# Two attention blocks on one core: the place of the softmax inverses, of one weight copy and of the output fetches

## Chip, core and metric

The kernel runs on one core of a Trainium2 chip. The metric is the device time of one execution in microseconds, as the median of several runs.

## The reference

Four images of 32 x 32 positions with 768 channels go through two layers of the same kind. All is in float32. In each layer:

```
x = x + attention(group_norm(x, groups=32))
attention:  q, k, v = x @ Wqkv (+ bias in layer 1), 12 heads of 64
            scores = scale * q k^T + rel_h[q_row, k_row] + rel_w[q_col, k_col]
            out = softmax(scores) v;   out @ Wproj + bproj
```

`rel_h` and `rel_w` are products of q with a small table of relative positions. Layer 1 scales q twice and has biases on q, k and v.

## The kernel before, in words

**Tiling.** The work is eight images (layer, image), each of six pairs of heads, each pair of eight steps. So there are 48 pairs g = 0 to 47, and pair number `pair` = g % 6 within its image. A step handles 128 query positions of both heads: a tile of scores of 128 x 1024 per head. Channels and positions are held transposed (channels on partitions) in 128 x 512 tiles.

**One step n of pair g**, in program order, with the lines of the profile:

- SP first issues what was put off from earlier steps (weight loads L131, stores L637); in pair 4 of an image also the loads of the next image (L117); in steps 4 and 6 `fetch` brings output weights `wo` (L580) and operands `res` (L600).
- GpSimd adds the two position terms of step n+2 into `sc` (L461).
- TensorE makes the scores of step n+1 (L475, eight records of the profile), VectorE adds them to `sc` and takes the row's maximum (L484), ACT takes the exponential and its sum (L488).
- SP reads back transposed weights of an earlier quarter (`pt<-td`, L526).
- VectorE transposes the two tiles of step n in 32 x 32 blocks (L515, `turn`), into tiles `tb`, of which there are three. After every second step (a quarter of the pair) SP writes them to DRAM (`td<-tb`, L518).
- VectorE takes the inverse of the sums of step n+1 (L495); GpSimd multiplies head 0's tile by it (L499), ACT head 1's (L501). This is `divide`.
- In pair 4 VectorE applies the norm to the next image's tiles (`apply`, L228).
- `take` issues the step's share of other TensorE work from a list `todo`: the projections of the next pair to q and k (L268) and values (L376), and output projections (L621).
- One function of the list `last`, if there is one: eight ACT copies of position terms into `rel` (L431), which read tiles `t` of the same pool as `res` (four tiles).
- After step 6 TensorE weighs the values with quarters 0 and 1 (L545, `weigh`), after step 2 with quarters 2 and 3 of the pair before.

**Projection of q and k.** In 39 of the 48 pairs (not the first of an image, nor pair 1) it is a product of 2 x 2 blocks with fewer block products. Of the weights, `w0` holds A11 (upper 64 rows, `TOP`) and A12 (`LOW`), `w1` A21 and A22, each in six chunks. ACT and GpSimd make S1 and S2 in `w3` (L324, L327, L328) and overwrite A21 (L329), in the steps before. Four units follow: unit 0 (six chunks, A11 and A12) in step 0, unit 1 (three chunks, S2, its two halves on the two halves of the array) and unit 2 (six chunks, S1 and S4) in step 1, unit 3 in step 3. Unit 1 finds chunks 0 to 2 of S2 in the place of A11's chunks 0 to 2, and unit 2 finds S4 = A12 - S2 in A12's place. So A11 and A12 are overwritten after unit 0 has read them, by the copy L336 on VectorE and the subtraction L337 on GpSimd:

```
def sum_weights_last(g):
    w0, w3 = w_of[g, 0], w_of[g, 3]
    nc.vector.tensor_copy(w0[TOP, :3], w3[LOW, :3])
    nc.gpsimd.tensor_tensor(w0[LOW], w0[LOW], w3[LOW], ALU.subtract)
```

It is called when unit 0's six chunks are issued, behind the reading of their result: ACT's copy into k (L296) and VectorE's addition into q (L243). Results of the units, of the position products (L408, copied to `t` by ACT, L418), of the weighing (L554, L557) and of the output products lie in two tiles of PSUM that are used in turn.

**What sets the order.** Each engine works through its own instructions in program order, and so does SP's DMA queue; waits are on semaphores. The order is written out by hand: the shares of each step stand in a list, for instance 6, 9, 0, 6, 6, 6, 0, 12 chunks for steps 0 to 7, and `first` says how many of them come ahead of the transposes.

Of the kernel before, what the change touches and what calls it, by code (L numbers as in the profile page):

```python
# [44 lines left out]
ALU = mybir.AluOpType  # L45
# [6 lines left out]
NC = C // P  # L52
NT = S // P
# [13 lines left out]
def attention_blocks(ctx: ExitStack, tc: tile.TileContext, a: dict, out: bass.AP):  # L67
    nc = tc.nc
# [27 lines left out]
    NPAIR = NI * NP  # L96

    w_of, wo_of = {}, {}
# [138 lines left out]
    def plain(g):  # L237
        return g % NP == 0 or g == 1
# [8 lines left out]
    def project_in(g, unit):  # L247

        im, pair = divmod(g, NP)
        xs, ys = x_of[im], y_of[im]  # L250
        if unit == 0:
            for which in range(2):
                tag = "qk"[which]
                qk_of[g, which] = qkpool.tile([P, S], FP, tag=tag, name=f"{tag}_{g}")
        if plain(g):
            which, i = divmod(unit, 2)
            w, x = 2 * [w_of[g, which]], xs[i * NC : (i + 1) * NC]
        else:
            w0, w1, w3 = w_of[g, 0], w_of[g, 1], w_of[g, 3]
            w, x = (  # L260
                ((w0, w0), xs[:NC]), ((w0, w3[:, 3:]), ys[NC:]),
                ((w3, w0), xs[NC:]), ((w1, w1), ys[:NC]),
            )[unit]
        t = ps_m.tile([P, 2, HALF], FP, tag="m", name=f"pj_{g}_{unit}")
        for c in range(len(x)):
            for a in range(2):
                rows = slice(a * D, (a + 1) * D)
                nc.tensor.matmul(  # L268
                    t[:, a, :], lhsT=w[a][rows, c, :], rhs=x[c][rows, :],
                    start=(c == 0), stop=(c == len(x) - 1),  # L270
                )
            if c < len(x) - 1:
                yield True

        q = [
            qk_of[g, 0][:, i * HALF : (i + 1) * HALF].rearrange("p (m a) -> p m a", a=4)
            for i in range(2)
        ]
        k = qk_of[g, 1].rearrange("p (a m) -> p a m", a=4)
        k = [k[:, :, i * P : (i + 1) * P] for i in range(2)]  # L280
        u = [t[:, a, :].rearrange("p (m a) -> p m a", a=4) for a in range(2)]
        t = [x.rearrange("p m a -> p a m") for x in u]
        bias = [None, None]
        if images[im][0]:
            bias = [bqkv[:, which, pair : pair + 1] for which in range(2)]
        if plain(g):
            to = k[i]
            if which == 0:
                to, t = q[i], u
            if images[im][0] == 0:  # L290
                nc.scalar.copy(to, t[0])
            else:
                nc.scalar.activation(to, t[0], AF.Identity, bias=bias[which])
            add(to, t[1], to)
        elif unit == 0:
            nc.scalar.copy(k[0], t[0])  # L296
            add(q[0], u[1], k[0].rearrange("p a m -> p m a"), bias[0])
            sum_weights_last(g)
        elif unit == 1:
            add(k[0], t[0], k[0])  # L300
            add(k[0], t[1], k[0])
        elif unit == 2:
            add(k[1], t[0], k[0])
            add(q[1], u[1], k[1].rearrange("p a m -> p m a"), bias[0])
        else:
            add(k[1], t[0], k[1], bias[1])
            add(k[0], t[0], k[0], bias[1])
            nc.vector.tensor_tensor(k[0], k[0], t[1], ALU.subtract)
        if unit in ((0, 1) if plain(g) else (0, 2)):
            (later if g else mid).append(lambda: positions(g, 1 if unit else 0))  # L310
        if g + 1 < NPAIR:
            if unit == (1 if plain(g) else 2):
                later.append(lambda: load_w(g + 1, 0))
            if unit == 3:
                early.append(lambda: load_w(g + 1, 1))
        yield True

    def sum_weights(g):

        w0, w1 = w_of[g, 0], w_of[g, 1]  # L320
# [12 lines left out]
    def sum_weights_last(g):  # L333

        w0, w3 = w_of[g, 0], w_of[g, 3]
        nc.vector.tensor_copy(w0[TOP, :3], w3[LOW, :3])  # L336
        nc.gpsimd.tensor_tensor(w0[LOW], w0[LOW], w3[LOW], ALU.subtract)  # L337

    def sum_input(im, n):

# [111 lines left out]
    sc_of, st_of, tb_of, pt_of, attn_of = {}, {}, {}, {}, {}  # L452
# [15 lines left out]
    def scores(g, n):  # L468
# [13 lines left out]
        for h in range(2):  # L482
# [7 lines left out]
                accum_out=st[:, 1, h : h + 1],  # L490
            )

    def divide(g, n):
        st = st_of[g, n]
        nc.vector.reciprocal(st[:, 2, :], st[:, 1, :])  # L495
        for h in range(2):
            sc = sc_of[g, n, h].rearrange("p k j -> p (k j)")
            if h == 0:
                nc.gpsimd.tensor_scalar(sc, sc, st[:, 2, h : h + 1], 1.0, ALU.mult, ALU.mult)  # L499
            else:  # L500
                nc.scalar.activation(sc, sc, AF.Copy, scale=st[:, 2, h : h + 1])  # L501

    def turn(g, n):

        quarter, j = divmod(n, 2)  # L510
        for h in range(2):
            if j == 0:
                tb_of[h] = tbpool.tile([P, HW, 2, HW], FP, tag="tb", name=f"tb_{g}_{n}_{h}")
            tb = tb_of[h]
            nc.vector.transpose(tb[:, :, j, :], sc_of[g, n, h])  # L515
            if j == 1:
                td = dram2.tile([P, S * 2], FP, tag=f"td{h}", name=f"td_{g}_{n}_{h}")
                nc.sync.dma_start(out=td, in_=tb.rearrange("p k n i -> p (k n i)"))  # L518
                (behind if quarter % 2 else behind2).append(
                    lambda queue=None, h=h, td=td: read_back(g, quarter, h, td, queue)  # L520
                )

    def read_back(g, quarter, h, td, queue=None):
        pt = ptpool.tile([P, 4, NT, 2 * HW], FP, tag=f"pt{h}", name=f"pt_{g}_{quarter}_{h}")
# [48 lines left out]
    def fetch(upto):  # L573

        while fetched[0] <= min(upto, len(parts) - 1):
            im, p, o, i = parts[fetched[0]]
            c0, c1 = cuts(im)[p : p + 2]
            if i == 0:
                w = wopool.tile([P, NC // 2, P], FP, tag="wo", name=f"wo_{im}_{p}_{o}")
                nc.sync.dma_start(  # L580
                    out=w[:, : c1 - c0, :],
                    in_=a[f"wo{images[im][0]}"][o][:, c0 * P : c1 * P].rearrange(
                        "p (c o) -> p c o", o=P
                    ),
                )
                for c in range(c0, c1):
                    wo_of[im, o, c] = w[:, c - c0, :]
            fetched[0] += 1
        while fetched[1] <= min(upto, len(parts) - 1):
            im, p, o, i = parts[fetched[1]]  # L590
            l, b = images[im]
# [21 lines left out]
    def project_out(im, p, o, i):  # L613
        l, b = images[im]
        end = im + 1 == NI
# [23 lines left out]
            nc.sync.dma_start(out=dst, in_=to)  # L639
        if i == 1 and (im, p, o, i) in place:  # L640
            if end and o > 1:
                fetch(place[im, p, o, i] + 4)
        yield True

# [37 lines left out]
    with tc.manual_schedule(engines=ENGINES):  # L682
# [19 lines left out]
        run(later)  # L702
        biases(0, 0)
        scores(0, 0)
        divide(0, 0)
        biases(0, 1)

        units = [(g, n) for g in range(NPAIR) for n in range(NT)]
        for at, (g, n) in enumerate(units):
            im, pair = divmod(g, NP)  # L710
# [18 lines left out]
            if pair == 4 and not end:  # L729
                if n == 0:  # L730
                    make_room(im + 1)
                for c in range(3 * n - 3, 3 * n) if 1 <= n <= 4 else ():
                    load_x(im + 1, c % NC, c // NC)
            if (im, pair) == (B - 1, 4) and n in (5, 7):
                (load_table if n == 5 else scale_table)(1)
# [1 line left out]
            early, later = later, early  # L737

            upto = 4 * (pair % 3) + 3
            if n in (4, 6) and (im, pair) >= (0, 3):  # L740
                upto -= 6 - n
                fetch(place[((im, 0) if pair >= 3 else (im - 1, 1)) + divmod(upto, 2)])

            ask = [divmod(g + 3, NP)] if n == 1 else []
            if im == 0 and pair < 3:
# [13 lines left out]
            if pair == 3 and n in stages and not end:  # L759
                stages[n]()  # L760
            share = shares[n]
            first = 3 if n == NT - 1 else 2 if end and pair == NP - 1 and n in (3, 4) else 0
            first = min(first, share)
            take(todo, first)
            share -= first
# [1 line left out]
            if at + 1 < len(units):  # L767
                divide(*units[at + 1])
            if pair == 4 and not end:
                for c in {2: (0, 1), 4: (2, 3), 6: (4, 5, 6, 7), 7: range(8, NX)}.get(n, ()):  # L770
                    if n == 7 and c % 2 == 0:
                        take(todo, 3)
                        share -= 3
                    apply(c % NC, c // NC)
# [2 lines left out]
                    combine = sum_weights(g + 2)  # L777
                combine[n - 6]()
            take(todo, share)
            if last:  # L780
                last.pop(0)()
            if pair == NP - 2 and n == 7 and not end:
                sum_input(im + 1, -1)
# [73 lines left out]
```

## Time and profile before

| what | value |
|---|---|
| median of three runs | 3571.03 us (3569.75 to 3577.24) |
| the profiled execution | 3578.79 us, of which 3577.0 us are the span of its instructions |
| ACT, busy | 1986.2 us |
| scores L475, eight records a step | 3072 records, 746.3 us |
| products L268 | 4140 records, 938.7 us |
| copy L336 | 39 copies, 25.2 us |
| inverse L495 | 384, mean 125 ns |
| transposes L515 | 768, mean 1222 ns |
| additions L461 on GpSimd | 768, mean 2083 ns |
| granted clock of TensorE | 0.994 of full speed |
| DMA | 1051.55 MB, mean 294 GB/s |

Busy times and waits are totals over the span. A line of a timeline gives the start, the duration, the engine, the line of the kernel, and at its end in brackets the idle time before it and what ended it. `PEld` is the loading of weights into TensorE, `SPq` an instruction of SP's queue. Matmuls are pipelined, so the times between their starts say more than their durations. Times within a pair are counted from the start of its step 0, and a step starts with the first of its eight score matmuls.

### The profile page before, as it was taken

To read this page: it belongs to the slowest core of one execution; us is meant where nothing else is said; L and a number is where in the kernel's file an instruction comes from. 1 tells how busy PE (TensorE), PEld (TensorE's weight loads), DVE (VectorE), ACT (ScalarE), POOL (GpSimd) and SP (SyncE) were. 2 spreads that over 40 slices of the span, in tenths; PEclk is the share of its full clock that TensorE was granted. 3 is DMA by queue.
4 is the path that set the end of the run, shared out by engine and by line. 5 is a ranking of instruction groups with operands and counts; after the bars stand their busy time and mean duration, and the time that the engine had idled before them with its cause. 6 is when DMAs were issued, how large, how long until landed. Compare 5 with 4: busy or idle time off the path is not lost.

```text
span 3577.0 us, 56189 instructions
## 1 busy us (share of the span) xinstructions
PE 3417.6 (96%) x20652; PEld 1897.0 (53%) x20652; DVE 2592.0 (72%) x4011; ACT 1986.2 (56%) x3958; POOL 2492.1 (70%) x1510
## 2 busy tenths in 40 slices
PE   6899999999999999999999999999999999999999
PEld 4455555555555556555555555555555555555554
DVE  4687867777777777777777777777766677776776
ACT  3565565555555556555655566555654555555552
POOL 3877686676967669676786667876678666786663
PEclk9999999999999999999999999999999999999999
DMA  3688978888788887888888788878988789887878
GB/s 118 244 287 319 328 278 302 318 309 316 276 316 317 300 307 272 319 293 306 292 308 304 281 316 301 306 285 292 308 307 301 271 290 330 299 291 276 296 288 289
DMA packets 531220, 1051.55 MB, mean 294 GB/s; under 512 B 143872, under 2 KB 206848, under 8 KB 481792
## 3 DMA queue, kind: packets, MB, share of 16 engines
q1 hardware_dynamic: 476448, 1020.53, 79.3%
q10 hardware_dynamic: 54496, 27.43, 2.6%
q8 instruction: 162, 2.65, 0.3%
q14 instruction: 114, 0.93, 0.1%
HBM read 572.73 MB, written 475.10 MB: 293 GB/s over the span
## 4 chain that ended last, share of the span: by engine, by line
PE 52%; DVE 17%; DMA 15%; ACT 5%; issue 5%; POOL 4%; SPq 2%; ACTq 0%; DVEq 0%; POOLq 0%
PE pj L268 13%; PE av L545 12%; PE s L475 10%; PE o L621 10%; DVE tb L515 8%; DMA td<-tb 7%; DMA pt<-td 7%; PE pv L376 6%; DVE sc L484 5%; ACT sc L501 2%; PE tp L408 2%; POOL sc L461 2%; DVE x L228 1%; POOL x L346 1%; POOL x L351 1%
## 5 line engine op out<-in xcount | busy, mean ns | idle before, releaser
L461 POOL TENSOR_TENSOR sc<-rel,rel 128x1024 f32<-128x1024 f32 x768 | 1546.1, 2083 | 42.6 <-DMA rel<-tdr 35.8
L488 ACT ACTIVATE sc<-sc,sm 128x1024 f32<-128x1024 f32 x768 | 880.1, 1147 | 662.8 <-DVE sm L484 660.0
L499 POOL TENSOR_SCALAR sc<-sc,sm 128x1024 f32<-128x1024 f32 x384 | 435.5, 1134 | 934.4 <-DVE sm L495 926.4
L484 DVE CUSTOM_DVE_ANT_0 sc<-s,sc 128x1024 f32<-128x1024 f32 x768 | 908.7, 1220 | 214.1 <-PE s L475 164.9
L268 PE MATMUL pj<-x,w 64*128 64x512 f32 x4140 | 938.7, 598 | 99.3 <-DVE w L336 60.1
L515 DVE STREAM_TRANSPOSE tb<-sc 128x1024 f32<-128x1024 f32 x768 | 913.0, 1222 | 122.9 <-DMA td<-tb 122.8
L545 PE MATMUL av<-pt,v 128*64 128x256 f32 x6144 | 717.3, 385 | 41.0 <-DMA pt<-td 41.0
L475 PE MATMUL s<-k,q 64*128 64x512 f32 x3072 | 746.3, 596 | 6.2 <-DVE sm L484 6.1
L501 ACT ACTIVATE sc<-sc,sm 128x1024 f32<-128x1024 f32 x384 | 441.0, 1148 | 556.8 <-DVE sm L495 556.8
L268 PEld LDWEIGHTS pj<-x,w 64*128 64x128 f32 x4140 | 415.7, 189 | 600.2 <-issue 444.4
L545 PEld LDWEIGHTS av<-pt,v 128*64 128x64 f32 x6144 | 446.0, 138 | 341.4 <-DMA pt<-td 60.3
L376 PE MATMUL pv<-wv,x 64*128 64x256 f32 x4608 | 514.1, 376 | 0.0
L376 PEld LDWEIGHTS pv<-wv,x 64*128 64x128 f32 x4608 | 446.4, 187 | 92.2 <-issue 29.9
L621 PE MATMUL o<-attn,wo 128*128 128x512 f32 x1080 | 480.5, 598 | 8.5 <-DVE attn L554 3.5
L475 PEld LDWEIGHTS s<-k,q 64*128 64x128 f32 x3072 | 289.2, 187 | 297.0 <-issue 272.7
L431 ACT COPY rel<-t 32x64 f32<-32x64 f32 x1504 | 362.9, 241 | 15.4
L621 PEld LDWEIGHTS o<-attn,wo 128*128 128x128 f32 x1080 | 199.9, 190 | 285.9 <-issue 234.4
L418 ACT COPY t<-tp 128x512 f32<-128x512 f32 x188 | 110.0, 585 | 191.5 <-PE tp L408 137.0
L243 DVE TENSOR_TENSOR k<-pj,k 128x512 f32<-128x512 f32 x173 | 116.8, 684 | 136.8 <-PE pj L268 94.9
L346 POOL TENSOR_TENSOR x<-x,x 64x512 f32<-64x512 f32 x144 | 182.6, 1288 | 43.9 <-ACT x L348 28.8
L391 DVE TENSOR_TENSOR v<-pv,v 128x256 f32<-128x256 f32 x192 | 81.4, 424 | 91.2 <-ACT v L388 88.0
L488 ACT ACTIVATION_READ_ACCUMULATOR sc<-sc,sm 128x1 f32 x768 | 143.2, 187 | 0.0
(54 smaller groups left out, 1516.9 us busy)
## 6 DMA issues: line engine op xcount, KB each, us to landing
td<-tb SPq DMA_DIRECT2D x384, 1024.0 KB, 5.6
pt<-td SPq DMA_DIRECT2D x382, 1024.0 KB, 8.0
w<-in_wqk SPq DMA_DIRECT2D x96, 384.0 KB, 3.5
tdr<-t ACTq DMA_DIRECT2D x94, 256.0 KB, 4.6
x<-in_x SPq DMA_DIRECT2D x84, 256.0 KB, 6.6
part<-res SPq DMA_DIRECT2D x84, 256.0 KB, 5.5
res<-part SPq DMA_DIRECT2D x84, 256.0 KB, 6.9
wv<-in_wv SPq DMA_DIRECT2D x24, 768.0 KB, 12.1
```

The costliest lines, as they stand in the source:

```text
L268: nc.tensor.matmul(t[:, a, :], lhsT=w[a][rows, c, :], rhs=x[c][rows, :], start=(c == 0), stop=(c == len(x) - 1),)
L376: nc.tensor.matmul(t[:, a, k, :], lhsT=xs[i // 2 * NC + c][rows, at * P : (at + 1) * P], rhs=w[rows, c, :], start=(c == 0), stop=(c == NC ...
L431: nc.scalar.copy(rel[of, :, j, :], t[of, j, :, at : at + HW])
L461: nc.gpsimd.tensor_tensor(sc.rearrange("p (a k) (u l) -> p a l (k u)", a=4, l=8), rel0[:, h, :].unsqueeze(1).unsqueeze(2).to_broadcast(shape),
L475: nc.tensor.matmul(ps[h][:, cols], lhsT=q[rows, n * P : (n + 1) * P], rhs=k[rows, cols], start=True, stop=True,)
L484: nc.vector.tensor_tensor_reduce(out=sc, in0=ps[h], in1=sc, scale=-scale, scalar=BIG, op0=ALU.add, op1=ALU.min, accum_out=st[:, 0, h : h + 1],
L488: nc.scalar.activation(sc, sc, AF.Exp, bias=st[:, 0, h : h + 1], scale=-1.0, accum_out=st[:, 1, h : h + 1],)
L499: nc.gpsimd.tensor_scalar(sc, sc, st[:, 2, h : h + 1], 1.0, ALU.mult, ALU.mult)
L501: nc.scalar.activation(sc, sc, AF.Copy, scale=st[:, 2, h : h + 1])
L515: nc.vector.transpose(tb[:, :, j, :], sc_of[g, n, h])
L545: nc.tensor.matmul(av[rows, at * 2 * P : (at + 1) * 2 * P], lhsT=v_of[g][:, k, rows], rhs=pt_of[g, quarter, h][:, :, k, :], start=(k == 0) ...
L621: nc.tensor.matmul(t, lhsT=wo_of[im, o, c], rhs=attn_of[im * NP + c, i], start=(c == c0), stop=(c == c1 - 1),)
```

## The change

Five things are moved; no arithmetic is added or removed. The weights are fetched by a function of their own.

- The inverse of step n+1 is taken between the two transposes of step n, no longer behind both.
- The copy of half of S2 over A11 is issued when three of unit 0's six chunks are, and those three now come ahead of step 0's transposes. The subtraction on GpSimd stays where it was.
- Output weights are fetched in step 2 (both of the pair), operands in steps 4 and 5, in place of both in 4 and 6.
- In step 3 two functions of `last` are run in place of one.
- In pair 4 the next image's tiles are loaded 6, 3 and 3 in steps 1, 2 and 4 (before: 3 each in 1, 2, 3, 4), and the norm is applied to 3, 1, 3 and 5 of them in steps 2, 4, 6, 7 (before: 2, 2, 4, 4).

```
@@ project_in
+            if c == 2 and unit == 0 and not plain(g):
+                nc.vector.tensor_copy(w0[TOP, :3], w3[LOW, :3])
...
         elif unit == 0:
             nc.scalar.copy(k[0], t[0])
             add(q[0], u[1], k[0].rearrange("p a m -> p m a"), bias[0])
-            sum_weights_last(g)
+            nc.gpsimd.tensor_tensor(w0[LOW], w0[LOW], w3[LOW], ALU.subtract)
@@ divide, turn
+    def invert(g, n):
+        st = st_of[g, n]
+        nc.vector.reciprocal(st[:, 2, :], st[:, 1, :])
+
     def divide(g, n):
         st = st_of[g, n]
-        nc.vector.reciprocal(st[:, 2, :], st[:, 1, :])
...
+            if h == 0 and g * NT + n + 1 < NPAIR * NT:
+                invert(*divmod(g * NT + n + 1, NT))
@@ main loop
-                for c in range(3 * n - 3, 3 * n) if 1 <= n <= 4 else ():
+                for c in {1: range(NC), 2: range(6, 9), 4: range(9, NX)}.get(n, ()):
                     load_x(im + 1, c % NC, c // NC)
...
-            if n in (4, 6) and (im, pair) >= (0, 3):
-                upto -= 6 - n
-                fetch(place[((im, 0) if pair >= 3 else (im - 1, 1)) + divmod(upto, 2)])
+            if n in (2, 4, 5) and (im, pair) >= (0, 3):
+                upto -= 2 if n == 4 else 0
+                (fetch_weights if n == 2 else fetch)(place[((im, 0) if pair >= 3 else (im - 1, 1)) + divmod(upto, 2)])
...
-            first = 3 if n == NT - 1 else 2 if end and pair == NP - 1 and n in (3, 4) else 0
+            first = 3 if n == NT - 1 or n == 0 and g + 1 < NPAIR and not plain(g + 1) else 2 if end and pair == NP - 1 and n in (3, 4) else 0
...
-                for c in {2: (0, 1), 4: (2, 3), 6: (4, 5, 6, 7), 7: range(8, NX)}.get(n, ()):
-                    if n == 7 and c % 2 == 0:
+                for c in {2: (0, 1, 2), 4: (3,), 6: (4, 5, 6), 7: range(7, NX)}.get(n, ()):
+                    if n == 7 and c % 2:
...
-            if last:
+            for k in range(min(len(last), 2 if n == 3 else 1)):
                 last.pop(0)()
```

More of the change, by code (lines that the diff above doesn't have):

```diff
@@ L331, in sum_weights @@
         return first, second
[L333 to L337, printed above, removed]
     def sum_input(im, n):
@@ L571, in attention_blocks, with fetch_weights @@
     fetched = [0, 0]
-    def fetch(upto):
+    def fetch_weights(upto):
         while fetched[0] <= min(upto, len(parts) - 1):
@@ L588, in fetch @@
             fetched[0] += 1
+    def fetch(upto):
         while fetched[1] <= min(upto, len(parts) - 1):
@@ L641, in project_out @@
             if end and o > 1:
+                fetch_weights(place[im, p, o, i] + 4)
                 fetch(place[im, p, o, i] + 4)
@@ L704, in attention_blocks @@
         scores(0, 0)
+        invert(0, 0)
         divide(0, 0)
```

## The prediction

> **What bounds the kernel now.** I read the page first, then the table of waits, then one ordinary pair of heads (g = 13) instruction by instruction, then the stretches in which the granted clock falls.
>
> ```profile
> PE 3417.6 (96%) x20652; PEld 1897.0 (53%) x20652; DVE 2592.0 (72%) x4011; ACT 1986.2 (56%) x3958; POOL 2492.1 (70%) x1510
> ```
>
> TensorE is the bound, and no other engine is above 72%. Its work is not changed here, so only its gaps can be won. The table of waits (total us, times, longest us) names two that recur:
>
> ```profile
> PEld pj L268 <- DVE w L336: 92.4, 39, 5.2
> ...
> PE pj L268 <- DVE w L336: 60.1, 39, 4.4
> ...
> PE av L545 <- DMA pt<-td: 41.0, 34, 2.7
> ```
>
> The first two lines are one wait, seen at the weight load and at the matmul: the product of unit 1 waits for the copy of half of S2 over A11 (L336). The third is the weighing of the values in step 6, which waits for the transposed weights to come back from DRAM. The TensorE timeline of pair 13 shows what the first is worth:
>
> ```profile
> 1018.42 1.88 PE L475 MATMUL s<-k,q 64*128 64x512 f32 x8
> 1021.66 8.00 PE L268 MATMUL pj<-x,w 64*128 64x512 f32 x36 [1.36 <-DVE w L336]
> 1029.49 1.06 PE L408 MATMUL tp<-tab,q 64*128 64x128 f32 x16
> ```
>
> Starts are the measure. Step 0 of this pair (8 + 24 records) takes 6.97 us, 0.218 us a record; so the products could start at 1018.42 + 8 x 0.218 + 0.01 = 1020.17. They start at 1021.66: 1.49 us lost, not 92.4/39 = 2.37, since a weight load would run ahead. VectorE and GpSimd at that time:
>
> ```profile
> 1015.87 2.37 DVE L515 STREAM_TRANSPOSE tb<-sc 128x1024 f32<-128x1024 f32 x2
> 1018.16 0.12 DVE L495 RECIPROCAL sm<-sm 128x2 f32<-128x2 f32 x1
> 1019.97 1.05 DVE L243 TENSOR_TENSOR q<-pj,k 128x512 f32<-128x512 f32 x1 [1.69 <-ACT k L296]
> 1021.05 0.56 DVE L336 COPY w<-w 64x384 f32<-64x384 f32 x1
> ```
>
> ```profile
> 1014.28 4.01 POOL L461 TENSOR_TENSOR sc<-rel,rel 128x1024 f32<-128x1024 f32 x2
> 1018.38 1.12 POOL L499 TENSOR_SCALAR sc<-sc,sm 128x1024 f32<-128x1024 f32 x1
> 1019.59 1.81 POOL L337 TENSOR_TENSOR w<-w,w 64x768 f32<-64x768 f32 x1
> ```
>
> The copy stands behind a chain: both transposes, inverse, ACT's multiplication, ACT's copy of k, the addition into q.
>
> The wait in step 6: it starts at +49.47 us of the pair and takes 8.87 us where nothing is late (pair 19). Over all pairs the steps 6 sum to 73 us above that: about 38 in the 40 ordinary pairs, 35 in the seven pairs (4, 10, ..., 40) that load the next image. Excess and landing agree: pair 13's second `pt` of quarter 1 lands 27.83 us after step 3's start and the excess is 1.94; pair 19's lands at 25.88, excess 0. What stands before it on SP's queue:
>
> ```profile
> 1047.39 7.41 SPq L447 DMA_DIRECT2D rel<-tdr  x8
> 1054.91 0.39 SPq L131 DMA_DIRECT2D w<-in_wqk  x1
> 1055.34 0.43 SPq L580 DMA_DIRECT2D wo<-in_wo  x1
> 1055.81 0.90 SPq L600 DMA_DIRECT2D res<-part  x2
> 1056.76 0.98 SPq L526 DMA_DIRECT2D pt<-td  x2
> ```
>
> **The change, part by part.** The orders of TensorE's and GpSimd's instructions are the same in both kernels; those of VectorE, ACT and SP differ.
>
> *Copy of the half (39 pairs).* It now waits for the third product of unit 0 and stands before the transposes. That product's last record starts 1.82 + 11 x 0.218 = 4.22 us into step 0 and takes 0.59, so the copy can start at +4.87; VectorE's L484s end at +4.50. It costs nothing new (0.39 to 2.74 us, median 0.50, in the rows of L336), only its place: waiting behind it are the transposes, the inverse and what depends on them. Here a rule speaks against the place. The Trainium skill (SBUF — State Buffer, Who interferes with whom) says that a VectorE copy in a 2-port mode and a GpSimd instruction exclude each other, and the later one blocks fully. The rows agree: 2742 ns in pair 2, across two L461s. At +4.87 GpSimd is in its second L461 (+4.78 to +6.84; some 1.1 us earlier once the inverse of the step before is early, so to about +5.75). By the median row the copy ends at +5.4, by the rule at +6.05; I take the rule. Transpose +7.3, inverse +7.4, ACT's multiplication +8.5, k +9.1, q +10.2, L337 (L499, then itself) +10.4. Unit 1 starts free at +8.7, unit 2 at +11.3 (it needs q's buffer and L337): covered by 0.9 us. The position products at +16.6 need unit 1 evacuated, at about +16.2: 0.4 us of cover, partly eaten. So 1.4 of the 1.49 us: 29 pairs x 1.4 = 40 us. In the seven pairs that start an image, GpSimd's two L461s end near +8.8; by the rule the copy ends at +7.1 and L337 at +12.1, 0.8 too late: 7 x 0.7 = 5 us (by the median row 10). Pairs 1 to 3 wait for GpSimd's L337 anyway: 2 us. Sum 47; bounds 25 and 56.
>
> *Inverse between the transposes (384 x 0.125 us).* It passes one transpose of 1.22 us: ACT and GpSimd get it some 1.1 us earlier; the second transpose waits for the second exponential's sum, 0 to 0.3 us per step by pair 13's rows. TensorE waits for neither; the gain is inside the numbers above. In step 6 the inverse no longer stands behind the transpose that waits for a `tb` buffer (122.8 us in 41 waits), so the next GpSimd additions are out of the way when the norm is applied.
>
> *Weights in step 2, operands in 4 and 5, both rel copies in step 3.* Ahead of `pt` one weight DMA goes: 0.43 us of SP and 192 KB, at the 235 GB/s that follows there 0.8 us. Against it the later second transpose of step 3, 0.25. The two `res` of step 5 stand behind `pt` and before `td` of quarter 2 (0.5 MB, 1.5 to 2.1 us): that makes the `tb` wait longer, for `pt` of quarter 2 is not needed until step 2 of the next pair. In step 2 the weights find SP idle. ACT's eight more copies in step 3 (8 x 0.25 = 2 us) delay the exponential and T in step 4 by about 1 us, under VectorE's 1.5 us of idle time there. Landing 0.5 us earlier (bounds +0.3 later, 0.8 earlier): 12 us in some 28 pairs that wait more than that, 4 in the seven; bounds -8 and 22.
>
> *Loads and the norm (seven pairs).* Loads 6, 3, 0, 3 in place of 3, 3, 3, 3: the three that stand before quarter 1's `pt` remain. Three L228 in step 2: alone 0.52 us, but 2.26 beside an L461 (rows of L228). With the inverse early they meet both L461s and hold back the evacuation L554 to about +31.8 (now +28.6), which unit 3 needs at +30.5: 1.3 us lost, 9 us in all (bounds 0 and 12). In step 6 three L228 in place of four, with GpSimd mostly done: step 7 is 14.4 us in five of these pairs and 15.7 in pair 4, against 12.4 undisturbed; I take 10 of these 12 us back. The wait in step 6 also costs clock:
>
> ```profile
> 1720.00:1723.00 3.00, 0.89 (x4) 0.42 (x6) 0.26 (x1) 0.75 (x2) 0.49 (x1) 0.92 1.09 427
> 1723.00:1726.00 3.00, 3.00 (x16) 1.66 (x14) 0.47 (x1) 0.00 (x0) 0.00 (x0) 0.51 0.98 407
> ```
>
> The seventh column is the granted clock: 3.4 us at half, 1.7 us lost, in six of the seven pairs; pair 4, with 2.2 us of wait, keeps it. I take 3 us back of 10. Last, in pairs before an image's first, unit 3 waits 0.5 us in step 4 for ACT's L418, behind GpSimd's sums: 3 us.
>
> **Sum**: 47 + 12 + 4 - 9 + 10 + 3 + 3 = 70 us. The profiled execution took 3578.8 (3577.0 of span); the median shown is 3571.0, 0.2% less, and the difference is not in any row. 3571 - 70 = 3501.
>
> **Rivals.**
> (1) *GpSimd keeps the copy out*: in every pair it waits to +7.1 or beyond. For: the row of 2742 ns, and the rule. Against: after the second L461 GpSimd has only L499, which needs the inverse behind the copy. Then 0.7 us a pair, and the rest as above: 47 becomes 27; 3521, with the applied norm at its worse bound 3530.
> (2) *The wait for `pt` goes too*: its queue empties by more than I count (SP's issues of 1.2 us each behind `td` show back-pressure), and step 6 gives 30 us more, with the clock 7 more: 3464.
> (3) *Slower: the `res` of step 5 share the DMA engines with `pt` of quarter 1 rather than follow it.* They are issued about 1 us after it and 9 us before it lands; shared, 0.5 MB at 235 GB/s is 2.1 us on 40 pairs, 84 us: 3585. It decides from 1.75 us (70/40) on. Against: all landings here are in order of issue (`w`, `wo`, `res`, `pt`, `td`).
> (4) *It does nothing*: what TensorE gains in step 1 comes back in step 6. Against: that chain starts with step 3's transposes, which move along with TensorE. About 3568.
>
> **Chances.** The sum as worked out (3480 to 3520) 0.52; rival 1 (to 3560) 0.23; rival 2 0.13; rival 4 0.05; rival 3 0.07. Range 3460 to 3545: it cuts off the far ends of rivals 1 and 2, and 3 and 4. A measurement of this kernel tells about 0.2% (7 us) from no change: faster 0.88, same 0.05, slower 0.07.
>
> **What would show it.** Right: no wait of L268 for the copy but in pairs 1 to 3; step 1 near 10.5 us in place of 11.96; quarter 1's `pt` landing half a us earlier after step 3; a longer wait of L515 for `td`; step 3 of the loading pairs longer than 6.87, their step 7 near 12.4. Wrong: a wait of L268 for L337, L243 or L336 in ordinary pairs, or a step 6 above 10.4 us on average.

## The result and the profile after

The changed kernel takes 3511.37 us (median of four runs, 3505.53 to 3515.57) against 3571.8 us before (four runs; the 3571.03 further up is of three): a ratio of 0.9827, 95% interval 0.9808 to 0.9846. Its profiled execution takes 3509.05 us, of which 3507.3 are the span. The profiled execution of before was the slowest of its runs, so the spans differ by 69.7 us and the medians by 60.

The engine row of the page after:

```profile
PE 3404.6 (97%) x20652; PEld 1906.9 (54%) x20652; DVE 2640.3 (75%) x4011; ACT 1992.0 (57%) x3958; POOL 2489.6 (71%) x1510
```

TensorE is busy about as long as before (3417.6 us) in a shorter span. VectorE is busy 48 us longer although it has the same 4011 instructions: some of them now take longer (the copies by 13 us in sum, the inverses by 12, the norm and the transposes by 9 each). From the table of waits after (total us, times, longest us):

```profile
DVE sm L495 <- ACT sc L488: 172.4, 269, 6.3
...
DVE tb L518 <- DMA td<-tb: 143.8, 43, 6.9
...
PEld av L550 <- DMA pt<-td: 46.5, 46, 2.6
...
PE av L550 <- DMA pt<-td: 22.8, 22, 2.1
```

```profile
PEld pj L268 <- DVE w L274: 10.3, 3, 4.3
...
PE pj L268 <- DVE w L274: 7.8, 3, 3.5
```

The copy (L336 before, L274 now) is waited for 3 times in place of 39, in pairs 1 to 3. TensorE's wait for `pt` fell from 41.0 to 22.8 us. VectorE waits longer for the second exponential's sum and for a free `tb`. TensorE in pair 13:

```profile
1010.45 1.88 PE L475 MATMUL s<-k,q 64*128 64x512 f32 x8
1012.17 7.89 PE L268 MATMUL pj<-x,w 64*128 64x512 f32 x36
1019.89 1.11 PE L408 MATMUL tp<-tab,q 64*128 64x128 f32 x16
```

The products start 1.72 us after step 1's scores, 3.24 before, and have no gap ahead of them. The 36 records follow each other in 7.89 us in place of 8.00. VectorE and GpSimd in the same time:

```profile
1008.14 1.28 DVE L274 COPY w<-w 64x384 f32<-64x384 f32 x1 [0.16 <-PE pj L268]
1009.45 1.25 DVE L518 STREAM_TRANSPOSE tb<-sc 128x1024 f32<-128x1024 f32 x1
1010.62 0.12 DVE L495 RECIPROCAL sm<-sm 128x2 f32<-128x2 f32 x1
1010.67 1.22 DVE L518 STREAM_TRANSPOSE tb<-sc 128x1024 f32<-128x1024 f32 x1
1012.43 1.06 DVE L243 TENSOR_TENSOR q<-pj,k 128x512 f32<-128x512 f32 x1 [0.55 <-ACT k L299]
```

```profile
1005.19 4.02 POOL L461 TENSOR_TENSOR sc<-rel,rel 128x1024 f32<-128x1024 f32 x2
1010.85 1.12 POOL L502 TENSOR_SCALAR sc<-sc,sm 128x1024 f32<-128x1024 f32 x1 [1.64 <-DVE sm L495]
1012.05 1.81 POOL L301 TENSOR_TENSOR w<-w,w 64x768 f32<-64x768 f32 x1
```

The two L461s end at 1009.21 and the copy at 1009.42, 5.94 us into the pair. What is behind it (inverse, L301, q) is just early enough. On SP's queue in the same pair no output weights (`wo`) stand ahead of quarter 1's `pt` any more, and two `res` follow it:

```profile
1045.00 0.38 SPq L131 DMA_DIRECT2D w<-in_wqk  x1
1045.43 0.91 SPq L608 DMA_DIRECT2D res<-part  x2
1046.38 0.99 SPq L531 DMA_DIRECT2D pt<-td  x2
1047.47 1.45 SPq L608 DMA_DIRECT2D res<-part  x2
```

To see where the time went, the trace is cut at the first score record of each step, for all 48 pairs. Ordinary are the 21 pairs with nothing special; loading are pairs 4, 10, ..., 46 (the last of these eight loads nothing); pre-image are the seven before an image's first, with the plain projection; image-first are pairs 6, 12, ..., 42. The mean us of a step, before and after, and the change of the sum over the class:

| step | class | before | after | sum, us |
|---|---|---|---|---|
| 1 | ordinary (21) | 11.96 | 10.37 | -33.2 |
| 1 | loading (8) | 11.95 | 10.33 | -12.9 |
| 1 | image-first (7) | 11.87 | 10.74 | -7.9 |
| 3 | loading | 6.87 | 7.93 | +8.5 |
| 4 | pre-image (7) | 12.80 | 13.10 | +2.1 |
| 5 | pre-image | 6.90 | 8.03 | +7.9 |
| 6 | ordinary | 10.15 | 9.31 | -17.6 |
| 6 | loading | 13.33 | 12.13 | -9.6 |
| 7 | loading | 13.99 | 13.18 | -6.5 |

The other classes and steps, with pairs 0 to 3 and 47, sum to within 1 us of nothing. These are single executions, and step 6 scatters: between two kernels that do not differ there, its sum changed by up to 3.8 us over the ordinary pairs and by up to 7.4 over the loading pairs. The other rows repeat within some 2 us.

### The profile page after: what moved, and what is told of

Read it like the earlier page. It is cut to its first block, busy times and chain, and to the rows that moved or that the text cites. A ratio compares the mean times of both kernels' runs of the same rounds, so it can differ in the third digit from the quotient of the medians.

```text
span 3507.3 us, 56203 instructions
## 1 busy us (share of the span) xinstructions
PE 3404.6 (97%) x20652; PEld 1906.9 (54%) x20652; DVE 2640.3 (75%) x4011; ACT 1992.0 (57%) x3958; POOL 2489.6 (71%) x1510
## 4 chain that ended last, share of the span: by engine, by line
PE 66%; ACT 12%; DMA 8%; DVE 6%; POOL 3%; issue 3%; SPq 1%; ACTq 0%; DVEq 0%; POOLq 0%
PE pj L268 17%; PE av L550 14%; PE s L475 13%; PE o L629 13%; PE pv L376 7%; ACT sc L488 6%; DMA pt<-td 5%; ACT rel L431 3%; ACT sc L504 2%; PE tp L408 2%; DMA td<-tb 2%; DVE x L228 1%; DVE sc L484 1%; DVE tb L518 1%; POOL x L346 1%
## 5 line engine op out<-in xcount | busy, mean ns | idle before, releaser
L461 POOL TENSOR_TENSOR sc<-rel,rel 128x1024 f32<-128x1024 f32 x768 | 1553.3, 2086 | 110.3 <-DVE tb L518 67.6
L518 DVE STREAM_TRANSPOSE tb<-sc 128x1024 f32<-128x1024 f32 x768 | 944.8, 1234 | 145.4 <-DMA td<-tb 143.8
L550 PE MATMUL av<-pt,v 128*64 128x256 f32 x6144 | 707.5, 383 | 22.8 <-DMA pt<-td 22.8
L376 PE MATMUL pv<-wv,x 64*128 64x256 f32 x4608 | 515.1, 376 | 6.8 <-DVE k L243 6.8
L376 PEld LDWEIGHTS pv<-wv,x 64*128 64x128 f32 x4608 | 449.5, 187 | 98.1 <-issue 38.0
L431 ACT COPY rel<-t 32x64 f32<-32x64 f32 x1504 | 363.4, 242 | 16.5
L495 DVE RECIPROCAL sm<-sm 128x2 f32<-128x2 f32 x384 | 60.1, 156 | 176.4 <-ACT sc L488 172.4
```

The costliest lines, as they stand in the source:

```text
L376: nc.tensor.matmul(t[:, a, k, :], lhsT=xs[i // 2 * NC + c][rows, at * P : (at + 1) * P], rhs=w[rows, c, :], start=(c == 0), stop=(c == NC ...
L431: nc.scalar.copy(rel[of, :, j, :], t[of, j, :, at : at + HW])
L461: nc.gpsimd.tensor_tensor(sc.rearrange("p (a k) (u l) -> p a l (k u)", a=4, l=8), rel0[:, h, :].unsqueeze(1).unsqueeze(2).to_broadcast(shape),
L550: nc.tensor.matmul(av[rows, at * 2 * P : (at + 1) * 2 * P], lhsT=v_of[g][:, k, rows], rhs=pt_of[g, quarter, h][:, :, k, :], start=(k == 0) ...
```

## The experiments

Theory: the copy must come early and the inverse too. A copy on VectorE is held until GpSimd's L461s are done, and only the early inverse keeps what stands behind it in time. The fetches clear the way for `pt`; the losses come from two pieces of VectorE and ACT work in places without cover. Rivals: the copy's place alone is the gain, or the early inverse alone. In each comparison the kernel before ran on the same chip (median 3576.8 us beside the four single parts, 3577.5 beside the undoings up to the second weight load, 3577.6 beside the rest). The changed kernel ran only for the result, so what an undoing gives is read from the steps.

### Each part alone

**The copy alone**, in the kernel before:

```diff
+            if c == 2 and unit == 0 and not plain(g):
+                nc.vector.tensor_copy(w0[TOP, :3], w3[LOW, :3])
...
-            sum_weights_last(g)
+            nc.gpsimd.tensor_tensor(w0[LOW], w0[LOW], w3[LOW], ALU.subtract)
...
-            first = 3 if n == NT - 1 else 2 if end and pair == NP - 1 and n in (3, 4) else 0
+            first = 3 if n == NT - 1 or n == 0 and g + 1 < NPAIR and not plain(g + 1) else 2 if end and pair == NP - 1 and n in (3, 4) else 0
```

> Kernel before with the copy of half of S2 alone moved (issued at unit 0's third chunk, those three chunks ahead of step 0's transposes). My theory: the early inverse is needed to bring GpSimd's two L461 of step 0 forward; without it the second L461 runs to +6.84, the copy ends at about +7.1 and L337 at +11.5 just misses unit 2 at +11.3, and unit 1's evacuation misses the position products at +16.6. Step 1 of ordinary pairs 10.9 to 11.2 us (before 11.96, after 10.37); in the seven pairs that start an image no gain. 26 us less: 3545 (3538 to 3552). Rival, the parts are independent and the copy alone brings the whole gain of step 1 (55 us): step 1 at 10.4, 3517.

Measured: 3582.37 us, ratio 1.0013 (1.0002 to 1.0024). Both expectations missed: there is no gain at all, and step 1 of ordinary pairs takes 12.02 us. (Lines of this kernel: scores L477, copy L273, L461 is L463, the subtraction L300.) The row of the copy among the groups, then pair 13 on VectorE, GpSimd and TensorE:

```profile
L273 DVE COPY w<-w 64x384 f32<-64x384 f32 x39 | 78.4, 2010 | 19.8 <-POOL w L331 13.9 <-PE pj L268 4.8 <-issue 1.1
```

```profile
1023.15 2.38 DVE L273 COPY w<-w 64x384 f32<-64x384 f32 x1 [0.16 <-PE pj L268]
1025.57 2.37 DVE L517 STREAM_TRANSPOSE tb<-sc 128x1024 f32<-128x1024 f32 x2
1027.86 0.12 DVE L497 RECIPROCAL sm<-sm 128x2 f32<-128x2 f32 x1
1029.67 1.04 DVE L243 TENSOR_TENSOR q<-pj,k 128x512 f32<-128x512 f32 x1 [1.69 <-ACT k L298]
```

```profile
1021.33 4.00 POOL L463 TENSOR_TENSOR sc<-rel,rel 128x1024 f32<-128x1024 f32 x2
1028.08 1.12 POOL L501 TENSOR_SCALAR sc<-sc,sm 128x1024 f32<-128x1024 f32 x1 [2.76 <-DVE sm L497]
1029.29 1.81 POOL L300 TENSOR_TENSOR w<-w,w 64x768 f32<-64x768 f32 x1
```

```profile
1027.18 2.74 PE L268 MATMUL pj<-x,w 64*128 64x512 f32 x12
1030.76 5.80 PE L268 MATMUL pj<-x,w 64*128 64x512 f32 x24 [0.84 <-DVE q L243]
1036.78 1.16 PE L410 MATMUL tp<-tab,q 64*128 64x128 f32 x16 [0.22 <-DVE k L243]
```

The copy takes 2.38 us: the second L463 ends at 1025.33, the copy at 1025.53. It delays both transposes and the inverse by 2.6 us, GpSimd sits idle for 2.76 us, L300 ends at 1031.10. Unit 1 is no longer late, but 12 records on, unit 2 waits 0.84 us for the addition into q, which frees its buffer, and the position products (L410) behind it wait for k on the late VectorE. Over all pairs there are some 30 waits of each kind: they have taken the place of the wait for the copy.

**The inverse alone**, in the kernel before:

```diff
@@ divide
+    def invert(g, n):
+        st = st_of[g, n]
+        nc.vector.reciprocal(st[:, 2, :], st[:, 1, :])
...
-        nc.vector.reciprocal(st[:, 2, :], st[:, 1, :])
@@ turn
+            if h == 0 and g * NT + n + 1 < NPAIR * NT:
+                invert(*divmod(g * NT + n + 1, NT))
...
```

> Kernel before with the inverse alone moved between the two transposes. My theory: ACT's copy of k and the addition into q come some 0.45 us earlier, so the copy at its old place does too: step 1 at 11.5 (before 11.96), 16 us; step 7 of the loading pairs 5 us; 3551 (3542 to 3560). Rival, TensorE waits for nothing behind the inverse: 3571. Second rival, the second transpose, kept back by the exponential's sum, makes quarter 1 late: step 6 longer by 0.3 us, 3580.

Measured: 3531.19 us, ratio 0.9868 (0.985 to 0.9886). This is the largest single part, over twice the 20 us expected. The copy at its old place comes earlier, since ACT's k and q in front of it do (pair 13: it starts 8.89 us into the pair, 9.60 before; 0.45 us were expected). TensorE's wait for it, 60.1 us before, is about halved:

```profile
PE pj L268 <- DVE w L336: 32.5, 39, 3.5
```

Step 1 falls to 11.13 us in ordinary pairs, half of the way; and 11.2 us come from step 7 of the loading pairs, 5.3 from step 4 of the pre-image pairs.

**The fetches and the double function of `last` alone**, and **the loads and the norm alone** (the diff's lines of `fetch`, `last`, `load_x` and `apply`):

> Kernel before with only the fetches moved (weights in step 2, operands in 4 and 5) and two functions of the list last run in step 3. My theory: step 6 of ordinary pairs falls by 0.5 to 0.8 us (15 us in all), and ACT's eight more copies in step 3 cost the pairs before an image's first 1.1 us in step 5 and 0.3 in step 4 (10 us): 3566 (3558 to 3574). Rival, the loss in those pairs comes from the inverse, which now waits for ACT's sum ahead of the second transpose: then it is absent here, 3556.

> Kernel before with only the loads (6, 3, 3 in steps 1, 2, 4) and the places of the norm (3, 1, 3, 5 in steps 2, 4, 6, 7) changed. My theory: the 8.5 us that step 3 of the loading pairs lost comes of the early inverse and the three L228 together; with the inverse late, the first L228 finds GpSimd idle and step 3 stays at 6.9 to 7.1. Step 7 gains about 0.6 us in seven pairs: 3567 (3562 to 3572). Rival, three L228 in step 2 are too many by themselves: step 3 at 7.9, 3576.

Measured: 3576.71 us, ratio 1.0 (0.999 to 1.001), and 3571.37 us, ratio 0.9984 (0.9976 to 0.9993). The fetches (3566 expected) do take 32.1 us out of steps 6, more than expected, but give back 14.8 in step 7 of the loading pairs, which was not foreseen, 7.9 in step 5 of the pre-image pairs and 3.4 in step 0 of the first four. The loss of 7.9 is there with the inverse at its old place, so the rival that blames the inverse falls. The loads win 12.6 us in step 7, and without the early inverse the three L228 in step 2 cost nothing in step 3, as expected.

The spans of the four single kernels are 0.4, 45.4, 5.3 and 9.8 us under that of before, 60.9 together; the whole change gives 69.7. By medians, each against before on its chip, the parts give 45 us together and the whole 60. Step 1 shows where the parts meet: over ordinary and loading pairs the copy alone gives 0.9 us, the inverse alone 24.0, the whole change 46.1, while fetches and loads leave it as it was. So no part but the inverse is worth much alone, and the VectorE copy gets its worth from the inverse.

### The copy on another engine

In the kernel before, the copy alone at its new place, but as an ACT instruction:

```diff
+            if c == 2 and unit == 0 and not plain(g):
+                nc.scalar.copy(w0[TOP, :3], w3[LOW, :3])
```

with the other lines as in the first experiment.

> The kernel before with the copy of the half alone at its new place, but done by ACT instead of VectorE; the inverse stays behind the transposes. Theory A (what cost the VectorE copy alone its gain is that GpSimd's second L461 keeps it out until +7.0): ACT's copy, behind its exponentials, runs from about +5.7 to +6.3 of the pair, transposes, inverse and k stay where they were, step 1 of ordinary pairs falls from 11.96 to about 10.5; -50 us, 3524. Theory B (the early place itself, ahead of unit 0's other work, without the early inverse wins nothing): step 1 stays at 12.0; 3577.

Measured: 3524.5 us, ratio 0.9854 (0.9836 to 0.9872); step 1 of ordinary pairs takes 10.33 us. This is theory A: 53 us less than before on the same chip, 50 expected. The row of the copy, and ACT in pair 13 (exponentials L490, multiplication L503):

```profile
L273 ACT COPY w<-w 64x384 f32<-64x384 f32 x39 | 19.9, 510 | 11.0 <-POOL w L331 10.1
```

```profile
1013.05 1.15 ACT L490 ACTIVATE sc<-sc,sm 128x1024 f32<-128x1024 f32 x1
...
1014.32 0.51 ACT L273 COPY w<-w 64x384 f32<-64x384 f32 x1
1015.38 1.15 ACT L503 ACTIVATE sc<-sc,sm 128x1024 f32<-128x1024 f32 x1 [0.55 <-DVE sm L497]
```

The same copy beside the same GpSimd additions takes 510 ns on ACT in the mean and 2010 on VectorE. It stands in a gap of ACT, so the transposes and the inverse stay where they were, and step 1 of ordinary pairs is as short as with the whole change (10.37), without the early inverse. In the image-first pairs it is not (11.68, against 10.74): there TensorE waits some 0.55 us for GpSimd's subtraction L300. So the early place by itself is not what made the VectorE copy worthless: it is what the copy met on VectorE, GpSimd's additions ahead of it and the transposes and the inverse behind it.

### The losses undone

**One function of `last` in step 3 of pre-image pairs**, else the changed kernel:

```diff
-            for k in range(min(len(last), 2 if n == 3 else 1)):
+            for k in range(min(len(last), 2 if n == 3 and not (g + 1 < NPAIR and plain(g + 1)) else 1)):
```

> Kernel after, but two functions of the list last in step 3 only where the next pair's projection is not a plain one, so one as before in the pairs before an image's first. My theory: ACT, late by some 6 us there behind GpSimd's sums, gets its eight copies back to step 4; step 5 of those seven pairs returns from 8.03 to 6.9 and step 4 from 13.1 to 12.8: 10 us less than after, 3501. Rival, the inverse ahead of the second transpose is what holds unit 3's evacuation there: no change, 3511.

Measured: 3501.05 us, ratio to before 0.9788 (0.9767 to 0.9808). Over the seven pairs steps 4 are 1.7 us shorter and steps 5 are 7.9, as expected. Pair 17 of the changed kernel, ACT and then TensorE:

```profile
1316.21 0.62 ACT L353 COPY x<-x 64x512 f32<-64x512 f32 x1 [2.79 <-POOL x L351]
...
1323.24 0.56 ACT L294 COPY k<-pj 128x512 f32<-128x512 f32 x1
1323.71 4.07 ACT L431 COPY rel<-t 32x64 f32<-32x64 f32 x16
1327.80 1.15 ACT L488 ACTIVATE sc<-sc,sm 128x1024 f32<-128x1024 f32 x1
...
1331.46 0.56 ACT L294 COPY k<-pj 128x512 f32<-128x512 f32 x1
```

```profile
1330.17 1.88 PE L475 MATMUL s<-k,q 64*128 64x512 f32 x8
1332.81 5.45 PE L376 MATMUL pv<-wv,x 64*128 64x256 f32 x48 [0.75 <-DVE k L243]
```

ACT waits for GpSimd's sums of the next image's input (L351) and is late, as in the kernel before; VectorE waits 6.24 us for its exponential there (the row of L495 in step 4). ACT's 16 copies (4.07 us) put the next exponential, the inverse and the copy of k behind them; VectorE's addition into k comes after that, and the values (L376) wait for the PSUM that k leaves. With eight copies the same two places read:

```profile
1319.42 2.02 ACT L431 COPY rel<-t 32x64 f32<-32x64 f32 x8
...
1325.12 0.57 ACT L294 COPY k<-pj 128x512 f32<-128x512 f32 x1
```

```profile
1325.88 1.88 PE L475 MATMUL s<-k,q 64*128 64x512 f32 x8
1327.60 5.35 PE L376 MATMUL pv<-wv,x 64*128 64x256 f32 x48
```

There k is copied 0.76 us before the scores of step 5, with 16 copies 1.29 us behind them.

**The norm in steps 2, 4, 6, 7 as 2, 2, 3, 5 tiles**, and **the last three loads in step 5, behind `pt`**:

```diff
-                for c in {2: (0, 1, 2), 4: (3,), 6: (4, 5, 6), 7: range(7, NX)}.get(n, ()):
+                for c in {2: (0, 1), 4: (2, 3), 6: (4, 5, 6), 7: range(7, NX)}.get(n, ()):
```

```diff
-                for c in {1: range(NC), 2: range(6, 9), 4: range(9, NX)}.get(n, ()):
+                for c in {1: range(NC), 2: range(6, 9), 5: range(9, NX)}.get(n, ()):
```

> Kernel after with the norm applied to 2, 2, 3, 5 tiles in steps 2, 4, 6, 7 (after: 3, 1, 3, 5). My theory: step 3 of the loading pairs returns from 7.93 towards 6.9, since the evacuation L559 comes one L461 earlier: 8 us less, 3503. Rival, the second L228 in step 4 meets GpSimd too and holds back the reading of scores in steps 5 and 6: what step 3 gains is lost in steps 5 to 7, 3511.

> Kernel after with the last three loads of the next image in step 5 in place of step 4, so behind quarter 1's pt on SP's queue. Theory that the place in the queue decides the wait of step 6: 0.75 MB ahead of pt go, some 3 us at 235 GB/s, of the 3.3 us of wait in the loading pairs: step 6 there from 12.1 to about 9.5, 18 us less, 3493. Rival, the landing of quarter 1's td and not the queue decides: within 4 us of after.

Measured: 3504.33 us, ratio 0.979 (0.9772 to 0.9808), and 3507.81 us, ratio 0.9803 (0.9785 to 0.9821). The first takes step 3 of the loading pairs back to 6.87 (-8.5 us), and steps 4 to 7 of these pairs give nothing of it back (1.0 us less in sum), so its rival falls. The second missed: step 6 of the loading pairs gives 21.8 us, as its theory had it (the first `pt` is issued 2.7 us earlier there), and step 7 takes 21.7 back. The rival's number came (within 4 us of after), but not for the rival's reason, since step 6 did fall. Why step 7 took it back is in the VectorE rows of pair 28, first of the changed kernel, then of the kernel with the late loads:

```profile
2127.54 1.25 DVE L518 STREAM_TRANSPOSE tb<-sc 128x1024 f32<-128x1024 f32 x1 [6.05 <-DMA td<-tb]
2128.71 3.15 DVE L228 TENSOR_SCALAR x<-x,nrm 128x512 f32<-128x512 f32 x3
```

```profile
2128.43 1.25 DVE L518 STREAM_TRANSPOSE tb<-sc 128x1024 f32<-128x1024 f32 x1 [5.84 <-DMA td<-tb]
```

The transpose that waits for `td` of quarter 2 starts 60.97 us into the pair with the loads ahead of `pt`, 60.77 with the loads behind it. `td` stands behind the loads either way: the same bytes are ahead of it, and it, not `pt`, sets the end of step 7.

**The second weight load behind `pt` too**:

```diff
-                early.append(lambda: load_w(g + 1, 1))
+                later.append(lambda: load_w(g + 1, 1))
```

> Kernel after with the second weight load of the next pair (L131, 384 KB) in step 5 in place of step 4, behind quarter 1's pt. Theory of the queue: 384 KB at 235 GB/s is 1.6 us, so step 6 falls to 8.9 to 9.0 in ordinary pairs (after 9.31) and pairs that start an image (10.0), and by 1.6 in loading pairs: 9 + 8 + 11 = 28 us less, 3483. Rival, pt would only be issued when td has landed, and the weights fill that time: a few us, 3505 to 3511.

Measured: 3508.18 us, ratio 0.9805 (0.9789 to 0.9822). Missed, 28 us were expected: steps 6 shorten by 17.3 us, but step 7 of the loading pairs grows by 10.0, their step 3 by 3.2, steps 1 by 3.6. In the loading pairs it is the same trade; in ordinary pairs step 6 gives only 2.2 us, within its scatter. The theory of the queue fails there: with 384 KB less ahead of it the first `pt` still lands 7.9 us after its issue in the mean (8.0 in the changed kernel), and it is issued only 0.4 us earlier. The time lies in the rival's range, but the rival's reason fails too: `td` has landed 2.5 us before `pt` is issued.

**The operands of step 5 in step 6 again** (weights stay in step 2):

```diff
-            if n in (2, 4, 5) and (im, pair) >= (0, 3):
+            if n in (2, 4, 6) and (im, pair) >= (0, 3):
```

> The changed kernel with the two res of step 5 fetched in step 6 again. Theory: in the loading pairs the td of quarter 2 stands behind these res, so it lands 1.3 us earlier and step 7 shortens by about 1 us each, 8 us: 3503; ordinary pairs stay. Rival of the prediction (res of step 5 share the DMA engines with pt): step 6 of all pairs shortens, by up to 1 us each, 3475. If neither: 3511.

Measured: 3501.46 us, ratio 0.9788 (0.9769 to 0.9806). The theory's side: step 7 of the loading pairs falls from 13.18 to 12.63 us (-4.4 in sum; in pair 28 the `td` of quarter 2 lands 1.09 us earlier), while step 6 of ordinary pairs stays (9.31, 9.26). So the `res` issued behind `pt` do not hold `pt` up, but they do hold up `td`. The steps account for only 5.9 us of span; the rest of the median's 10 lies within the scatter of runs.

### Together

The changed kernel with the two undone losses, and the last loads in step 6, behind the `td` of quarter 2:

```diff
+                for c in {1: range(NC), 2: range(6, 9), 6: range(9, NX)}.get(n, ()):
...
+                for c in {2: (0, 1), 4: (2, 3), 6: (4, 5, 6), 7: range(7, NX)}.get(n, ()):
...
+            for k in range(min(len(last), 2 if n == 3 and not (g + 1 < NPAIR and plain(g + 1)) else 1)):
```

> The changed kernel with three edits: the second rel copy in step 3 left out in pairs before an image's first; the norm of the three tiles in steps 2, 3, 5 and 7 as in the second of the two single undoings; and the last three loads of the next image in step 6, behind the td of quarter 2, in place of step 4. Theory (each loss is its own; in the loading pairs what ends step 7 is the td of quarter 2, 0.5 MB of three loads ahead of it on SP's queue): -10 from step 5 of the pre-image pairs, -8 from step 3 of the loading pairs, -18 to -22 from their step 6, and step 7 not longer but 1 to 2 us shorter (td of quarter 2 lands near +59 instead of +61): 3511 - 45 = 3466. Rival (loads so late leave their norm late in step 7, or push pt of quarter 2): step 7 of the loading pairs grows by 2 to 3 us, about 3490.

Measured: 3488.48 us, ratio 0.9753 (0.9735 to 0.977). The first three terms came as expected (-7.9, -8.5, -20.0), the fourth did not: step 7 of the loading pairs grew by 9.4 us, the rival's mechanism at half its size (1.2 us a pair). Pair 28, VectorE and then TensorE:

```profile
2113.23 1.25 DVE L518 STREAM_TRANSPOSE tb<-sc 128x1024 f32<-128x1024 f32 x1 [0.96 <-DMA td<-tb]
2114.40 4.03 DVE L228 TENSOR_SCALAR x<-x,nrm 128x512 f32<-128x512 f32 x3
2118.35 0.86 DVE L562 TENSOR_SCALAR attn<-av,bqkv 128x256 f32<-128x256 f32 x2
```

```profile
2119.36 8.67 PE L629 MATMUL o<-attn,wo 128*128 128x512 f32 x18 [1.24 <-DVE attn L562]
```

The wait for `td` is 0.96 us in place of 6.05, but the three L228 now meet more of GpSimd's additions and take 4.03 us in place of 3.15; behind them stands the evacuation L562, for which the output products wait: 1.24 of the 2.2 us by which step 7 of this pair is longer.

With the operands of step 5 in step 6 as well (both diffs above):

> The three edits of the first kernel of this batch together with the res of step 5 fetched in step 6. Theory: the td of quarter 2 in the loading pairs has one megabyte less ahead of it than in the changed kernel, lands near +57.5; step 7 of these pairs near its 12.4: some 5 us under the first kernel of this batch, 3461. If the last wait in these pairs is then another (norm on VectorE beside GpSimd's L461), no difference between the two.

Measured: 3476.84 us, ratio 0.9725 (0.971 to 0.974), the fastest version, 1% under the changed kernel by the two ratios. Both of its expectations hold in part: in pair 28 nothing changes (the three L228 take 4.81 us there), but over the loading pairs step 7 falls from 14.35 to 13.76 us, 4.7 in sum.

## Why the prediction came out right, and what in it did not

The time of 3511.37 lies within the range, 10 us above the 3501 foretold. By medians 60 us went where 70 were foretold (55 to 69 by the interval of the ratio). The spans differ by 69.7, but that near hit is in part luck: the execution of before that was profiled was its slowest, and errors of the terms cancel. Step 1 and step 6 gave 16 us more than foretold; the pre-image pairs and step 7 of the loading pairs gave 16.5 less. Term by term:

| term of the sum | foretold | measured |
|---|---|---|
| step 1, 29 ordinary and loading pairs | 40 | 46.1 |
| step 1, image-first pairs | 5 | 7.9 |
| step 1, pairs 1 to 3 | 2 | 1.1 |
| step 6, ordinary | 12 | 17.6 |
| step 6, loading, with its clock | 4 + 3 | 9.6 |
| step 3, loading | -9 | -8.5 |
| step 7, loading | 10 | 6.5 |
| pre-image pairs, steps 4 and 5 | 3 | -10.0 |

**The copy.** The rule that the later of the two instructions is held was taken against the median row, and pair 13 bore it out: the copy ended 5.94 us into the pair, foretold 6.05 by the rule and 5.4 by the row. The sum also needed the early inverse for L461 to end in time, and the text said so. What it did not see is how much hung on that: the copy alone is worth nothing, and on ACT it is worth all of step 1 in ordinary and loading pairs. Rival 1 is true of the copy alone (kept out to +7.04), and false of the whole change. The term is 6 us too small: of the loss of 1.49 us only 1.4 were counted, for a wait of the position products that did not come, and the loss was read at unit 1's start alone. Step 1 shortened by 1.59; in pair 13 the 36 products themselves take 0.11 us less.

**The step that failed** is the one that hid ACT's eight more copies "under VectorE's 1.5 us of idle time there". Pair 13, an ordinary pair, has such idle time (1.47 us, ended by a copy of ACT), and in ordinary pairs the cover held: steps 4 and 5 stay at 6.90 us. In the pre-image pairs ACT is late already, and the same 2 us fell on the path: +2.1 in step 4, where -3 was foretold, and +7.9 in step 5, for which nothing was. Leaving them out gave 9.6 us back. The -3 was right for the inverse alone (-5.3), but it is missing from the whole change for another reason too: with the eight copies left out, step 4 still takes 12.86 us (12.80 before, 12.05 with the inverse alone). Which of the other parts takes it was not found.

**Step 6.** Over the ordinary pairs the second `pt` of quarter 1 lands 26.24 us after step 3's start in the mean, 27.15 before: 0.91 us earlier, 0.5 foretold. Pair 13, with 25.70 and 27.83, is an extreme; the loading pairs stayed late (pair 28: 29.94). The surplus may be scatter: in the four kernels of these experiments that keep the fetches and start from before, step 6 of the ordinary pairs is 3.7 to 8.3 us less than in before itself, so of the 17.6 us between 9 and 14 are the fetch, and 12 were foretold. That the size came right is in part luck. The prediction counted 0.43 us of SP and 0.8 us for 192 KB ahead of `pt`, less 0.25. The traces show SP's part: in the mean of the ordinary pairs the first `pt` is issued 15.55 us after step 3's start, 16.10 before, and it lands 8.0 us after its issue in both. In the other kernels, whatever stands ahead of it, that is 7.8 to 8.1 us. Rival 2 went too far: of 71 us by which step 6 exceeded 8.87 in ordinary, loading and image-first pairs, 43 are left.

**Step 7 of the loading pairs.** The wait of VectorE for `td` was foretold to grow and did (122.8 to 143.8 us), but it was priced at nothing because `pt` of quarter 2 is not needed soon. It is not `pt` that waits there, it is VectorE, with the norm and the evacuation L562 behind it. The fetches alone made this step 14.8 us longer in sum. Moving the `res` out of the way gave 4.4 us of step 7, about what was missing.

**The rivals.** The 3530 of rival 1 does not follow from the bounds given: 3521 and the 3 us to the norm's worse bound make 3524. The `res` of step 5 land behind `pt`: on SP's queue all 1886 transfers landed in order of issue, before and after. Step 6 of ordinary pairs is the same with and without them, so rival 3's mechanism is not there. Rival 4 fell with step 1.

**What stays open.** How much of the difference between the sum of the parts and the whole is scatter was not tried: each span is one profiled execution. The copy and the inverse were not run together without the other parts. The ACT copy was not run together with the rest of the change.

## What to carry to other kernels

An instruction that is moved costs what its neighbours in time make of it: before the move, look at which engine works at the new place, and whether a third engine has a gap there. Cover must be read in every kind of stage that the moved work runs in, not in the ordinary one; the special pairs were 14 of 48 and held all the losses. And when a wait is shortened by moving transfers on a queue, follow the queue to the next reader: in the loading pairs each microsecond taken from `pt` came back at `td` until the transfers were behind both.

## What the hardware showed that was not expected

- Where the VectorE copy met an instruction of GpSimd, it ended just after it. In the copy-alone kernel all 39 copies ended 0.21 to 0.22 us after one (31 after an addition L463, eight after an L348), and in the changed kernel 32 of 39. So the copy's duration says how much of that instruction was left; in the other seven only 0.10 to 0.12 us was left, and the copy took 0.36 us. On ACT all 39 took 509 to 511 ns. The Trainium skill (SBUF — State Buffer, Terms) says that VectorE and GpSimd share a port pair whose loser fully blocks, and that ACT has its own; the copies on both engines agree. Not every VectorE instruction is held: the two transposes of pair 13 before ran beside an L461 in 2.37 us.
- A copy that waited for the first of two adjoining additions never got in between them: in the copy-alone kernel twelve with 0.24 to 0.27 us of the first left, and pairs 2 and 3 with 1.95 us left, were held to the end of the second. Between L337 and L461 it did get in (29 copies of the kernel before). An L228 always got in between two L461s, in 14 of 14 such places of the changed kernel; in step 2 of pair 28 it was held for 2.3 us, and the two L461s then took 4.49 us together in place of 4.00. What decides that is not known from these runs.
- After the wait in step 6 of the loading pairs TensorE ran at half clock for about 3.4 us in six of them before the change, three after it, and none in the two kernels under "Together". In one of the three, the seventh column (granted clock) of a window of 4 us:

```profile
2124.00:2128.00 4.00, 4.00 (x26) 2.40 (x24) 0.46 (x1) 0.00 (x0) 0.71 (x1) 0.61 1.01 424
```
